# A perceiver layer with 16 experts: the next expert's tokens turned one piece earlier, the last bias added by VectorE, the gate as four column tiles

## The chip, the cores and the metric

The kernel is one program on one core of a Trainium2 chip. The core has five engines with queues of their own: TensorE (PE in the profile; its weight loads are listed as PEld), VectorE (DVE), ScalarE (ACT), GpSimd (POOL) and SyncE (SP), which issues most transfers. An engine works through its queue in order. Results of products land in PSUM, which has eight banks; everything else is in SBUF. The metric is the device time of one execution in microseconds (us); less is better.

## The reference

All values are float32. With `x` of 2 x 512 tokens by 512 and a context of 2 x 8192 by 512, the layer is three residual blocks:

```python
x = x + xattn(layernorm(x), ctx, mask)     # 16 heads over 8192 keys
x = x + window_attn(layernorm(x))          # 16 heads, 7 keys around each token
x = x + ffn(layernorm(x))                  # 16 experts and a shared block
```

The change is in the third. The tokens are flattened to `h`, 1024 x 512. Each of 16 experts picks the 128 tokens that score highest for it:

```python
scores = sigmoid(h @ gate_w.T)                    # 1024 x 16
topk_score, topk_ids = top_k(scores.T, 128)       # for each expert
xin = h[topk_ids]                                 # 16 x 128 x 512
up = einsum('ecd,efd->ecf', xin, up_w) + up_b     # f = 2048
g  = einsum('ecd,efd->ecf', xin, gw) + gb
eo = einsum('ecf,edf->ecd', silu(g) * up, down_w) + down_b
out = zeros.at[topk_ids].add(eo * topk_score)     # a token may be picked by several
shared = (silu(h @ sh_gate_w.T) * (h @ sh_up_w.T)) @ sh_down_w.T
ffn = out + shared
```

## The kernel before, in words

The program is written with tiles and pools. A planner orders the instructions of each engine: it takes them in the order of the source, but one that becomes ready early by its plan may move ahead of earlier source lines. It also puts in all waits. At run time each engine keeps the planned order. So the place of a line in the source is a priority and not a promise.

*Cross attention* (up to line 546) takes most of the span. It is not touched. Its products come in two tile shapes of TensorE that matter below: values `pv` and `av` use 128 rows by 32 columns, four such column tiles beside each other, each writing its own 32 partitions of PSUM; scores `sc` use 32 rows by 128 columns.

*Window attention* (lines 586 to 853) runs over 40 items, batch by head group by block of 103 queries. `beside` (line 776) hangs small work on these items: norms, the transposed `hT` of the tokens, and the preparation of biases. `picks` (784) makes `pick`, 16 blocks of 128 equal columns in which one row is 1 and the others 0. `bias_in` (790) loads `gb` and `up_b` into `rows` and three copies of `down_b` into `raw`; `bias_part` (806) splits `raw` into three bf16 parts, `bias3`, whose sum is the float32 value. So one bf16 product of `pick[:, e, :]` with `bias3` gives 128 equal rows of down's bias for expert e.

*Shared block and gate* (lines 919 to 960). For each batch, eight steps `f` make two products `pf` of 128 x 512 with `hT`, take Silu on ScalarE and multiply into `sT` on VectorE; then four products `pso` over the eight `sT` give the shared output. `gated` (861) runs for both batches after step 5 of batch 0: four products (one per 128 of the model's width) of `gate_sb`, 128 x 16, with 512 tokens, into the first 16 partitions of one bank `pg`, and one Sigmoid into `sc` (16 x 1024). `select` (877) then takes eight of the top 128 scores per call on VectorE, 16 calls hung between the steps; `turned_lists` (890) turns the lists into columns `idx` and `scol`.

*Experts* (lines 962 to 1020). One loop of 65 steps `k`: expert `e`, piece `fq` of four. `expert_in` (962) makes the two products of a piece, `gw` and `up`, each 4 x 4 matmuls of 128 x 128 x 128 into one bank, then four Silus on ScalarE and four joined add-and-multiply on VectorE into `eoT`. `expert_out` (986) of the expert before comes behind piece 0: the bias product (988), 16 matmuls of 512 columns with `down`'s four tiles (994), a multiply by the score column on VectorE (999), and on POOL an indirect transfer that adds the 128 rows to `out` (1000). `gather` (899) fetches the next expert's 128 rows `xin` on POOL in piece 0. `tokens` (908) turns them: `transposed` (95) makes four transposes on TensorE and one copy to `xinT` on ScalarE. Before the change `tokens` stands behind piece 3, so right ahead of the next expert's piece 0, which reads `xinT`.

Weights come through `load_tile` (551) on SyncE's queue: 1 MB each, 12 per expert, into nine buffers in turn (four of `ctx`, five of `w`). A load is issued when the buffer's former tile has been used. `xin`, `xinT`, `eoT`, `sg` and `y` have two buffers each. All results of products take turns in the eight banks of `ps`.

A float32 matmul appears as two records in the trace, a transpose or a bf16 matmul as one.

Of the kernel before, what the change touches and what calls it, by code (L numbers as in the profile page):

```python
# [10 lines left out]
F32 = mybir.dt.float32  # L11
I32 = mybir.dt.int32
U32 = mybir.dt.uint32
BF16 = mybir.dt.bfloat16
AF = mybir.ActivationFunctionType
ALU = mybir.AluOpType
# [3 lines left out]
P = 128  # L20
B, S, D = 2, 512, 512
# [4 lines left out]
DC = D // P  # L26
# [6 lines left out]
E, F, SH, CAP = 16, 2048, 1024, 128  # L33
FQ = F // 512
# [9 lines left out]
def perceiver_kernel(  # L44
# [8 lines left out]
    nc = tc.nc  # L53

    const = ctx.enter_context(tc.tile_pool(name="const", bufs=1))
    ident = const.tile([P, P], F32, name="ident")
# [38 lines left out]
    def transposed(dst, src, ps):  # L95

        tp = ps.tile([P, 4, P], F32, tag="ps", name="tp")
        for c in range(4):
            nc.tensor.transpose(tp[:, c, :], src[:, ts(c, P)], ident)  # L99
        nc.scalar.copy(dst, tp)  # L100
# [17 lines left out]
    with ExitStack() as es:  # L118
        cp = es.enter_context(tc.tile_pool(name="a_const", bufs=1))
        tmp = es.enter_context(tc.tile_pool(name="a_tmp", bufs=2))  # L120
# [8 lines left out]
        ps = first_ps.enter_context(tc.tile_pool(name="a_ps1", bufs=1, space=PSUM))  # L129
# [364 lines left out]
        for slot in range(NS + LAG):  # L494
            if slot == LAG:
                first_ps.close()
                ps = ps_q = es.enter_context(tc.tile_pool(name="a_ps", bufs=8, space=PSUM))
# [53 lines left out]
    def load_tile(src):  # L551
        pool, tag = ((ctxp, "ctx"), (wpool, "w"))[loads[0] % 9 >= 4]
        loads[0] += 1
        t = pool.tile([P, 4, 512], F32, tag=tag, name="wt")
        nc.sync.dma_start(out=t, in_=src)
        return t

    ccp = ctx.enter_context(tc.tile_pool(name="c_const", bufs=1))
    ctmp = ctx.enter_context(tc.tile_pool(name="c_tmp", bufs=2))
    ps = ctx.enter_context(tc.tile_pool(name="c_ps", bufs=8, space=PSUM))  # L560
# [2 lines left out]


    bias_c = ccp.tile([P, 4, P], F32, name="bias_c")


    KB3 = 96
    pick = ccp.tile([KB3, E, P], BF16, name="pick")
    bias3 = ccp.tile([KB3, D], BF16, name="bias3")  # L570
    gate_sb = ccp.tile([P, DC, E], F32, name="gate_sb")
    nc.gpsimd.dma_start(out=gate_sb, in_=gate.rearrange("(c p) e -> p c e", p=P))
    idx = ccp.tile([P, E], U32, name="idx")
    scol = ccp.tile([P, E], F32, name="scol")
# [8 lines left out]
    xnT, aT, hT = {}, {}, {}  # L583


    with ExitStack() as es:
        cp = es.enter_context(tc.tile_pool(name="b_const", bufs=1))
        tmp = es.enter_context(tc.tile_pool(name="b_tmp", bufs=2))
        gp = es.enter_context(tc.tile_pool(name="b_g", bufs=3))
        bp = es.enter_context(tc.tile_pool(name="b_bias", bufs=1))  # L590
# [12 lines left out]
        for h in range(4):  # L603
            r = slice(h * DK, (h + 1) * DK)
# [8 lines left out]
            out=band, in_=band, pattern=[[1, NK]], base=0, channel_multiplier=-1,  # L613
# [3 lines left out]
            out=band, in_=band, pattern=[[-1, NK]], base=W7 - 1, channel_multiplier=1,  # L617
# [3 lines left out]
        def attention_in(n, ln):  # L621
            b, m = divmod(n, NT // B)
            if m == 0:
                xnT[b] = batch_tile("xnT")
            xn = tmp.tile([P, D], F32, tag="row", name="xn")
            normalized(xn, n, *ln)
            transposed(xnT[b][:, :, ts(m, P)], xn, ps)
# [150 lines left out]
        def at(k, f, *args):  # L778
            beside.setdefault(k, []).append(lambda: f(*args))
# [1 line left out]
        def norm(b, key):  # L781
            lns[key] = layernorm_stats(lnp, range(b * (NT // B), (b + 1) * (NT // B)))

        def picks(i):
            r = ds(32 * i, 32)
            nc.vector.tensor_copy(
                pick[r], ident[r, ds(32 * i, E)].unsqueeze(2).to_broadcast([32, E, P])
            )

        def bias_in():  # L790
            rows = bp.tile([P, 4, P], F32, name="rows")
            for i, src in enumerate((gb, up_b)):
                nc.gpsimd.dma_start(
                    out=rows[:, ts(i, 2), :],
                    in_=src.rearrange("e (c p) -> (e c) p", p=P).rearrange("(n r) p -> r n p", r=P),
                )
            raw = bp.tile([KB3, D], F32, name="raw")
            nc.gpsimd.memset(raw, 0.0)
            for i in range(3):
                nc.gpsimd.dma_start(out=raw[ds(32 * i, E), :], in_=down_b)  # L800
            raws.extend((rows, raw))

        def bias_cols():
            transposed(bias_c, raws[0].rearrange("r n p -> r (n p)"), ps)

        def bias_part(i):
            raw = raws[1]
            part = bp.tile([KB3, D], BF16, name="part")
            nc.vector.tensor_copy(part, raw)
            r = ds(32 * i, 32)  # L810
            nc.vector.tensor_copy(bias3[r, :], part[r, :])
            if i < 2:
                nc.vector.tensor_tensor(raw, raw, part, ALU.subtract)

        def forward_in(n, key):

# [8 lines left out]
        lns, raws = {"b0": ln_b0}, []  # L825
        at(2, norm, 1, "b1")
        for i, k in enumerate((4, 6, 8, 10)):
            at(k, lambda n: attention_in(n, lns["b1"]), NT // B + i)
        for i in range(3):
            at(3 + 2 * i, picks, i)  # L830
        at(9, bias_in)
        at(13, bias_cols)
        for i in range(3):
            at(15 + 2 * i, bias_part, i)
        at(29, norm, 0, "f0")
        for i, k in enumerate((31, 33, 35, 37)):
            at(k, forward_in, i, "f0")
# [5 lines left out]
        for k in range(len(items) + 3):  # L843
            i, n = divmod(k, NBQ)
# [14 lines left out]
    sc = sp.tile([E, T], F32, name="sc")  # L859

    def gated(b):
        pg = ps.tile([P, S], F32, tag="ps", name="pg")
        for c in range(DC):
            nc.tensor.matmul(
                pg[0:E, :], lhsT=gate_sb[:, c, :], rhs=hT[b][:, c, :],
                start=(c == 0), stop=(c == DC - 1),
            )
        nc.scalar.activation(sc[:, ts(b, S)], pg[0:E, :], AF.Sigmoid)

# [27 lines left out]
    def gather(e):  # L899

        xin = ep.tile([P, D], F32, name="xin")
        nc.gpsimd.indirect_dma_start(  # L902
            out=xin, out_offset=None, in_=h_dram,
            in_offset=bass.IndirectOffsetOnAxis(ap=idx[:, e : e + 1], axis=0),
        )
        return xin

    def tokens(xin):
        xinT = ep.tile([P, DC, CAP], F32, name="xinT")
        transposed(xinT, xin, ps)  # L910
        return xinT
# [3 lines left out]
    tmp = ctmp  # L915
# [3 lines left out]
    for b in range(B):  # L919
        sT = sTp.tile([P, SH // P, S], F32, tag="sT", name="sT")  # L920
        for f in range(SH // P):
            pair = []
            for wts in (shg, shu):
                pf = ps.tile([P, S], F32, tag="ps", name="pf")
                for c in range(DC):
                    nc.tensor.matmul(  # L926
                        pf, lhsT=wts[f // 4][:, c, ts(f % 4, P)], rhs=hT[b][:, c, :],
                        start=(c == 0), stop=(c == DC - 1),
# [10 lines left out]
            elif b == 1 and f == SH // P - 1:  # L939

                turned_lists()
                xin = gather(0)
# [3 lines left out]
        for j in range(4):  # L946
            po = ps.tile([P, D], F32, tag="ps", name="pso")
            for f in range(SH // P):
                nc.tensor.matmul(  # L949
                    po, lhsT=sT[:, f, ts(j, P)], rhs=shd[f // 4][:, f % 4, :],  # L950
                    start=(f == 0), stop=(f == SH // P - 1),
# [10 lines left out]
    def expert_in(e, fq, xinT, eoT):  # L962

        pair = []
        for src in (gw, up):
            wt = ahead.pop(0) if ahead else load_tile(src[e, fq])
            pf = ps.tile([P, 4, CAP], F32, tag="ps", name="pf")
            for j in range(4):
                for c in range(DC):
                    nc.tensor.matmul(  # L970
                        pf[:, j, :], lhsT=wt[:, c, ts(j, P)], rhs=xinT[:, c, :],
                        start=(c == 0), stop=(c == DC - 1),
                    )
            pair.append(pf)
        sg = tmp.tile([P, 4, CAP], F32, name="sg")
        for j in range(4):
            i, k = divmod(e * (F // P) + fq * 4 + j, P)
            nc.scalar.activation(  # L978
                sg[:, j, :], pair[0][:, j, :], AF.Silu, bias=bias_c[:, i, k : k + 1]
            )  # L980
            nc.vector.scalar_tensor_tensor(  # L981
                eoT[:, fq * 4 + j, :], pair[1][:, j, :], bias_c[:, 2 + i, k : k + 1],
                sg[:, j, :], ALU.add, ALU.mult,
            )

    def expert_out(e, eoT):
        py = ps.tile([P, D], F32, tag="ps", name="py")
        nc.tensor.matmul(
            py, lhsT=pick[:, e, :], rhs=bias3, start=True, stop=False
        )  # L990
        for fq in range(FQ):
            wt = load_tile(down[e, fq])
            for c in range(4):
                nc.tensor.matmul(  # L994
                    py, lhsT=eoT[:, fq * 4 + c, :], rhs=wt[:, c, :],
                    start=False, stop=(fq == FQ - 1 and c == 3),
                )
        y = tmp.tile([P, D], F32, name="y")
        nc.vector.tensor_scalar(y, py, scol[:, e : e + 1], None, ALU.mult)  # L999
        nc.gpsimd.indirect_dma_start(  # L1000
            out=out, out_offset=bass.IndirectOffsetOnAxis(ap=idx[:, e : e + 1], axis=0),
            in_=y, in_offset=None, compute_op=ALU.add,
        )
# [3 lines left out]
    for k in range(E * FQ + 1):  # L1007
        e, fq = divmod(k, FQ)
        if e < E:
            if fq == 0:  # L1010
                eoT[e] = ep.tile([P, F // P, CAP], F32, name="eoT")
                if e > 0:
                    xinT = nxt
                if e + 1 < E:
                    xin = gather(e + 1)
            expert_in(e, fq, xinT, eoT[e])
        if fq == 0 and e > 0:
            expert_out(e - 1, eoT[e - 1])
        if fq == FQ - 1 and e + 1 < E:
            nxt = tokens(xin)  # L1020


# [47 lines left out]
```

## Time and profile before

| what | value |
|---|---|
| median of 3 runs | 3717.26 us (3716.56 to 3718.0) |
| the profiled execution's own time | 3718.25 us |
| its span (first to last instruction) | 3716.5 us |
| TensorE busy | 3669.1 us, 99% |
| VectorE / ScalarE / POOL busy | 2190.0 / 1705.4 / 2083.9 us |
| shared block and gate, on the chain | from about 2831 to 3006 us |
| experts, on the chain | from 3005.77 us to the end |
| weight loads of experts, issue to landing (median) | 5.3 us gw and up, 6.8 us down |
| traffic, expert stretch from 3034 to 3650 | 299 GB/s, transfer engines 87% busy |

The page gives busy times and a chain: the work that ended last, followed backwards to what released each step. A group line has the line of the kernel, engine, operation, result and operands, shape and count; behind the first bar busy time and the mean of one instruction in ns; behind the second the idle time of the engine just before, and what ended it. The chain in order of time has start, duration and what, with the count of instructions. The waits have the waiting line, what it waited for, then total us, times and the longest. Matmuls overlap in the pipeline, so the mean of one matmul is longer than its share of the time; the chain's durations add up.

### The profile page before, as it was taken

The page shows a single profiled execution, that of the slowest core. Times are in us where ns is not written, and L with a number is a line of the kernel's source. Part 1 is how long each engine was busy: PE and PEld are TensorE (multiplying, and loading weights), DVE is VectorE, ACT ScalarE, POOL GpSimd, SP SyncE. Part 2 cuts the span into 40 slices and gives each one's busy share as a digit, 9 for nine tenths or more (in the row PEclk, how much of TensorE's full clock was granted, in tenths as well). Part 3 has the DMA queues.
Part 4 walks back from the last instruction along what each step waited for, and adds up shares of the span by engine and source line. Part 5 has one row for each costly group of instructions (what it writes and reads, how often), then busy time and mean ns, then how long its engine had stood idle before and what let it go on. Part 6 is the DMA issues. An engine that isn't in the chain of part 4 may idle for free.

```text
span 3716.5 us, 108745 instructions
## 1 busy us (share of the span) xinstructions
PE 3669.1 (99%) x47424; PEld 2064.8 (56%) x47424; DVE 2190.0 (59%) x5333; ACT 1705.4 (46%) x3449; POOL 2083.9 (56%) x569
## 2 busy tenths in 40 slices
PE   8999999999999999999999999999999999999998
PEld 4555555555555555555555554444454478888776
DVE  7866667677666766767776676799653711111111
ACT  1145555555555555555555555688463001111110
POOL 0059989998998998999899899700100000000000
PEclk9999999999999999999999999999999999999999
DMA  6322222222224432221222122122201068888885
GB/s 206 104 71 66 73 73 65 66 73 73 65 67 123 124 118 92 73 73 63 69 73 73 61 70 73 61 89 76 76 15 55 34 240 302 299 300 298 300 296 185
DMA packets 145021, 437.88 MB, mean 118 GB/s; under 512 B 9392, under 2 KB 14544, under 8 KB 119200
## 3 DMA queue, kind: packets, MB, share of 16 engines
q1 hardware_dynamic: 139344, 419.20, 34.0%
q0 software_dynamic: 5200, 11.73, 1.2%
q8 instruction: 371, 6.08, 0.7%
q14 instruction: 106, 0.87, 0.1%
HBM read 422.43 MB, written 8.47 MB: 116 GB/s over the span
## 4 chain that ended last, share of the span: by engine, by line
PE 95%; issue 2%; ACT 1%; DMA 1%; POOL 1%; DVE 0%; SPq 0%; POOLq 0%; ACTq 0%
PE av L406 14%; PE sx L318 13%; PE sc L384 12%; PE pk L259 12%; PE pv L277 12%; PE pf L970 12%; PE py L994 6%; PE sc L390 3%; PE pf L926 3%; PE sx L299 2%; PE pqkv L644 2%; PE pso L949 1%; PE po L107 1%; PE pq L185 1%; ACT sb L720 1%
## 5 line engine op out<-in xcount | busy, mean ns | idle before, releaser
L418 POOL TENSOR_TENSOR acc<-acc,pt 128x2048 f32<-128x2048 f32 x437 | 1991.1, 4556 | 168.8 <-ACT pt L397 161.8
L323 DVE CUSTOM_DVE_ANT_0 junk<-sx,mk 128x512 bf16<-128x512 f32 x1776 | 1225.4, 690 | 628.8 <-PE sx L318 432.4
L397 ACT ACTIVATE pt<-sc,mbias 128x512 f32<-128x512 f32 x2016 | 1220.3, 689 | 788.4 <-PE sc L390 788.1
L277 PEld LDWEIGHTS pv<-wv_sb,ctx_t 128*32 128x32 f32 x16384 | 457.6, 110 | 176.5 <-DVE mst L323 103.3
L384 PE MATMUL sc<-qT,kt 32*128 32x512 f32 x4096 | 542.1, 595 | 0.0
L406 PE MATMUL av<-pt,vt 128*32 128x512 f32 x4032 | 539.6, 605 | 0.0
L318 PE MATMUL sx<-kt,qT 32*128 32x512 f32 x3552 | 508.0, 640 | 0.7 <-ACT vt L286 0.7
L277 PE MATMUL pv<-wv_sb,ctx_t 128*32 128x128 f32 x16384 | 500.1, 273 | 2.0 <-DVE avs L414 2.0
L259 PE MATMUL pk<-ctx_t,wk_sb 128*32 128x256 f32 (+1 forms) x9088 | 493.4, 357 | 1.3 <-DMA ctx_t<-in_ctxT 1.3
L970 PE MATMUL pf<-xinT,wt 128*128 128x128 f32 x4096 | 463.9, 275 | 10.1 <-ACT xinT L100 10.1
L970 PEld LDWEIGHTS pf<-xinT,wt 128*128 128x128 f32 x4096 | 461.0, 192 | 21.3 <-ACT xinT L100 13.7
L259 PEld LDWEIGHTS pk<-ctx_t,wk_sb 128*32 128x32 f32 x9088 | 280.6, 110 | 290.1 <-DVE mst L323 100.8
L414 DVE TENSOR_TENSOR avs<-av,avs 128x512 f32<-128x512 f32 x504 | 344.8, 684 | 2.0 <-PE av L406 2.0
L384 PEld LDWEIGHTS sc<-qT,kt 32*128 32x128 f32 x4096 | 234.7, 184 | 188.3 <-issue 111.0
L978 ACT ACTIVATE sg<-pf,bias_c 128x128 f32<-128x128 f32 x256 | 73.0, 368 | 566.3 <-PE pf L970 566.3
L981 DVE SCALAR_TENSOR_TENSOR eoT<-pf,bias_c,sg 128x128 f32<-128x128 f32 x256 | 72.1, 344 | 413.5 <-PE pf L970 413.5
L406 PEld LDWEIGHTS av<-pt,vt 128*32 128x32 f32 x4032 | 80.2, 108 | 323.0 <-DVE mst L323 277.8
L1000 POOL DMA_INDIRECT out_x<-y,idx x16 | 25.2, 1576 | 402.5 <-DVE y L999 402.5
L902 POOL DMA_INDIRECT xin<-h_dram,idx x16 | 15.8, 990 | 411.7 <-PE tp L99 286.6
L263 ACT ACTIVATE kt<-pk,bk_c 128x256 f32<-128x256 f32 (+1 forms) x284 | 128.1, 451 | 209.0 <-PE pk L259 209.0
L994 PE MATMUL py<-wt,eoT 128*128 128x512 f32 x512 | 222.3, 592 | 0.0
L318 PEld LDWEIGHTS sx<-kt,qT 32*128 32x128 f32 x3552 | 139.6, 183 | 135.3 <-issue 70.5
(177 smaller groups left out, 2360.5 us busy)
## 6 DMA issues: line engine op xcount, KB each, us to landing
ctx_t<-in_ctxT SPq DMA_DIRECT2D x159, 1024.0 KB, 6.4
wt<-in_gw SPq DMA_DIRECT2D x64, 1024.0 KB, 5.3
wt<-in_up SPq DMA_DIRECT2D x64, 1024.0 KB, 5.3
wt<-in_down SPq DMA_DIRECT2D x64, 1024.0 KB, 6.8
mk<-mrow SPq DMA_DIRECT2D x111, 256.0 KB, 3.5
ctx<-in_wqkv SPq DMA_DIRECT2D x3, 1024.0 KB, 5.2
mk<-mrow_h SPq DMA_DIRECT2D x16, 128.0 KB, 4.5
wt<-in_sh_d SPq DMA_DIRECT2D x2, 1024.0 KB, 4.8
```

The costliest lines, as they stand in the source:

```text
L259: nc.tensor.matmul(pk[ts(h, DK), :], lhsT=wk_sb[:, c, ds(g * P + h * DK, DK)], rhs=ctx_t[slot, b][:, c, hs], start=(c == 0), stop=(c == DC ...
L263: nc.scalar.activation(k_t[slot][:, hs], pk, AF.Identity, bias=bk_c[:, g : g + 1])
L277: nc.tensor.matmul(pv[ts(k, DK), i, :], lhsT=ctx_t[slot, b][:, c, ds((lo + i) * P + k * DK, DK)], rhs=wv_sb[:, c, ts(g, P)], start=(c == 0 ...
L318: nc.tensor.matmul(sm, lhsT=qT[r, g, ds(b * S + c * P, P)], rhs=k_t[s][r, :], start=True, stop=True)
L323: nc.vector.tensor_tensor_reduce(out=junk, in0=ss[h], in1=mk_t[s], scale=1.0, scalar=-3.0e38, op0=ALU.add, op1=ALU.max, accum_out=mst[u][: ...
L384: nc.tensor.matmul(sc, lhsT=k_t[s][r, ts(ch, P)], rhs=qT[r, g, ts(b, S)], start=True, stop=False)
L397: nc.scalar.activation(pt[:, h, :], ss[h], AF.Exp, bias=mbias[:, b, cc : cc + 1], scale=SCALE)
L406: nc.tensor.matmul(av[ts(h, DK), :], lhsT=v_t[s][:, ch, ts(h, DK)], rhs=pt_t[s, ch][:, h, :], start=True, stop=True,)
L414: nc.vector.tensor_tensor(avs[u], av, avs[u], ALU.add)
L418: eng.tensor_tensor(acc[u], acc[u], pt_t[s, ch], ALU.add)
L970: nc.tensor.matmul(pf[:, j, :], lhsT=wt[:, c, ts(j, P)], rhs=xinT[:, c, :], start=(c == 0), stop=(c == DC - 1),)
L994: nc.tensor.matmul(py, lhsT=eoT[:, fq * 4 + c, :], rhs=wt[:, c, :], start=False, stop=(fq == FQ - 1 and c == 3),)
```

## The change

Three edits go together.

1. `tokens(xin)` for the next expert stands in front of piece 3 instead of behind it.
2. `pick`, `bias3`, their preparation and the bias product go. `expert_out` loads down's bias of its expert as one row repeated to 128 partitions into `y` on SyncE's queue, VectorE multiplies it by the score column, and the last step becomes product times score plus `y`.
3. `gated` computes each batch as four groups of 128 tokens, each in its own 16 of 32 partitions of a 128 x 128 tile, and takes four Sigmoids per batch back into the 16 rows of `sc`.

```diff
-    KB3 = 96
-    pick = ccp.tile([KB3, E, P], BF16, name="pick")
-    bias3 = ccp.tile([KB3, D], BF16, name="bias3")
...
         def bias_in():
...
-            raw = bp.tile([KB3, D], F32, name="raw")
-            nc.gpsimd.memset(raw, 0.0)
-            for i in range(3):
-                nc.gpsimd.dma_start(out=raw[ds(32 * i, E), :], in_=down_b)
-            raws.extend((rows, raw))
+            raws.append(rows)
...
-        for i in range(3):
-            at(3 + 2 * i, picks, i)
         at(9, bias_in)
         at(13, bias_cols)
-        for i in range(3):
-            at(15 + 2 * i, bias_part, i)
...
     def gated(b):
-        pg = ps.tile([P, S], F32, tag="ps", name="pg")
+        pg = ps.tile([P, P], F32, tag="ps", name="pg")
         for c in range(DC):
-            nc.tensor.matmul(
-                pg[0:E, :], lhsT=gate_sb[:, c, :], rhs=hT[b][:, c, :],
-                start=(c == 0), stop=(c == DC - 1),
-            )
-        nc.scalar.activation(sc[:, ts(b, S)], pg[0:E, :], AF.Sigmoid)
+            for m in range(4):
+                nc.tensor.matmul(
+                    pg[ds(32 * m, E), :], lhsT=gate_sb[:, c, :], rhs=hT[b][:, c, ts(m, P)],
+                    start=(c == 0), stop=(c == DC - 1),
+                )
+        for m in range(4):
+            nc.scalar.activation(sc[:, ds(b * S + m * P, P)], pg[ds(32 * m, E), :], AF.Sigmoid)
...
     def expert_out(e, eoT):
         py = ps.tile([P, D], F32, tag="ps", name="py")
-        nc.tensor.matmul(
-            py, lhsT=pick[:, e, :], rhs=bias3, start=True, stop=False
-        )
+        y = tmp.tile([P, D], F32, name="y")
+        nc.sync.dma_start(out=y, in_=down_b[e].partition_broadcast(P))
+        nc.vector.tensor_scalar(y, y, scol[:, e : e + 1], None, ALU.mult)
         for fq in range(FQ):
             wt = load_tile(down[e, fq])
             for c in range(4):
                 nc.tensor.matmul(
                     py, lhsT=eoT[:, fq * 4 + c, :], rhs=wt[:, c, :],
-                    start=False, stop=(fq == FQ - 1 and c == 3),
-                )
-        y = tmp.tile([P, D], F32, name="y")
-        nc.vector.tensor_scalar(y, py, scol[:, e : e + 1], None, ALU.mult)
+                    start=(fq == 0 and c == 0), stop=(fq == FQ - 1 and c == 3),
+                )
+        nc.vector.scalar_tensor_tensor(y, py, scol[:, e : e + 1], y, ALU.mult, ALU.add)
         nc.gpsimd.indirect_dma_start(
...
                 if e + 1 < E:
                     xin = gather(e + 1)
+            if fq == FQ - 1 and e + 1 < E:
+                nxt = tokens(xin)
             expert_in(e, fq, xinT, eoT[e])
         if fq == 0 and e > 0:
             expert_out(e - 1, eoT[e - 1])
-        if fq == FQ - 1 and e + 1 < E:
-            nxt = tokens(xin)
```

More of the change, by code (lines that the diff above doesn't have):

```diff
@@ L782, in norm @@
             lns[key] = layernorm_stats(lnp, range(b * (NT // B), (b + 1) * (NT // B)))
[L784 to L787, printed above, removed]
-            )
         def bias_in():
@@ L796, in bias_in @@
                 )
-            raw = bp.tile([KB3, D], F32, name="raw")
-            nc.gpsimd.memset(raw, 0.0)
-            for i in range(3):
-                nc.gpsimd.dma_start(out=raw[ds(32 * i, E), :], in_=down_b)
-            raws.extend((rows, raw))
+            raws.append(rows)
         def bias_cols():
             transposed(bias_c, raws[0].rearrange("r n p -> r (n p)"), ps)
[L806 to L813, printed above, removed]
         def forward_in(n, key):
```

## The prediction

> **What bounds the kernel now.** I read the page first: busy shares, the slices with the clock, the chain by engine.
>
> ```profile
> PE 3669.1 (99%) x47424; PEld 2064.8 (56%) x47424; DVE 2190.0 (59%) x5333; ACT 1705.4 (46%) x3449; POOL 2083.9 (56%) x569
> PEclk9999999999999999999999999999999999999999
> PE 95%; issue 2%; ACT 1%; DMA 1%; POOL 1%; DVE 0%; SPq 0%; POOLq 0%; ACTq 0%
> ```
>
> TensorE is busy 99% of the span at the full clock and is 95% of the chain that ended last. So a change is worth what it takes from TensorE's own queue. All other engines count only where TensorE waits for them. Second, the chain in order of time over the experts (start, duration, what; each f32 product counts as two records). One period:
>
> ```profile
> 3034.35 0.45 PE tp L99 x4
> 3034.80 0.02 issue
> 3034.82 0.59 ACT xinT L100
> 3035.42 0.04 issue
> 3035.46 7.41 PE pf L970 x64
> 3042.87 0.22 PE py L988
> 3043.09 13.73 PE py L994 x32
> 3056.83 21.44 PE pf L970 x192
> ```
>
> It repeats every 43.92 us (the next turn starts at 3078.26). TensorE stands still once in it: between the four transposes and the next expert's first product, while ScalarE copies xinT. Third, the same view around two products of attention and around the gate:
>
> ```profile
> 2501.49 0.87 PE pv L277 x32
> 2502.36 1.07 PE sc L384 x8
> 2503.65 1.00 PE av L406 x8
> ```
>
> ```profile
> 2874.14 6.97 PE pg L864 x16
> 2881.11 13.93 PE pf L926 x32
> ```
>
> Around the gate TensorE has no gap. Last, the groups of instructions in the expert stretch, SyncE's waits there, its timeline, and TensorE's at the same time:
>
> ```profile
> L970 PE MATMUL pf<-xinT,wt 128*128 128x128 f32 x4094 | 463.7, 275 | 10.1 <-ACT xinT L100 10.1
> L988 PE MATMUL py<-bias,pick 96*128 96x512 bf16 x16 | 6.1, 381 | 0.0
> ```
>
> ```profile
> SPq L555 <- PE pf L970: 395.9, 119, 4.5
> SPq L555 <- PE py L994: 172.5, 56, 3.2
> ```
>
> ```profile
> 3056.86 11.05 SPq L555 DMA_DIRECT2D wt<-in_down  x4
> ```
>
> ```profile
> 3086.84 13.90 PE L994 MATMUL py<-wt,eoT 128*128 128x512 f32 x32
> ```
>
> SyncE waits only for TensorE to free a weight buffer, never TensorE for a transfer. The down tiles issued from 3056.86 are used from 3086.84: 30 us of lead against 6.9 us to land (median of those loads), so 23 us to spare.
>
> **Tokens in front of the last piece.** The step that moves is four transposes on TensorE and one copy on ScalarE; it issues no DMA. On TensorE it passes the 64 records of the last piece; on ScalarE, its four silus; nothing on SP. On POOL the gather two experts on waits for these transposes and starts some 7.1 us earlier. The transposes stay at 0.45 us. What goes is the stall: 0.02 + 0.59 + 0.04 = 0.65 us, and the refill behind it: 64 records took 7.41 us here, but 192 took 21.44, which is 7.15 per 64, so 0.26. Together 0.91 us, 15 times: **-13.7 us**. The copy (0.59) is then covered by the last piece's 7.15 us. Without that cover it costs the same 0.91 again. The gathered rows must be there earlier: those turned at 3078 were gathered at 2999.17, so nothing is late. Low end of the gain: the 10.1 us of idle time alone; high end 13.7, taken because the chain shows the refill in each period.
>
> **Down's bias on VectorE.** Gone are 16 products of 0.22 us on the chain: **-3.5 us** (6.1 by their busy time, but they overlap their neighbours). Added per expert:
> - SyncE issues one more load, one row repeated to 128x512, 256 KB. The nearest row is the mask's rows of the same size, 3.5 us to land. In transfer time: the hardware queue moved 419.20 MB in 34.0% of the span, 3.0 us per MB, so 0.8 us. The engines were busy 0.87 of 43.92 us, 38.2; with this, 39.0 of a new period of 42.78, 0.91. Below one, so nothing; it costs once the load takes over 4.6 us of all engines.
> - VectorE multiplies it by the score: 0.48 us (the 128x512 multiply from SBUF at L429) to 0.75 (L999, from PSUM). VectorE is busy 74 of 616 us there. This waits for the load, and the next piece's products into eoT queue behind it. Those are wanted a piece (7 us) later at the earliest, and two buffers of sg let ScalarE and TensorE run two pieces on, some 14 us. Nothing.
> - The last multiply becomes multiply and add. Only after the final expert is it on the path: 0.75 us at L999, against 0.69 for adding PSUM and SBUF at L111. Between -0.1 and +0.3; I take 0.
>
> Removed earlier: VectorE's picks (three of 1.2 us) and parts (3.5 us in all), POOL's memset and three loads, between 2612 and 2643. VectorE waited 0.48 us for ScalarE right behind the last of them, so they delay no one. TensorE stands still 3.0 us in all between 2632 and 2642, for copies and residuals, so another order of instructions there (the program orders itself by a plan) may be worth -3 to +3 us; I take 0, since no wait names a removed instruction.
>
> **Gate.** 16 records of 512 columns took 6.97 us. Now there are 64 of 128 columns in four column tiles. The nearest row is the value product, 128 rows by 32 columns by 128: 500.1 us for 16384, 30.5 ns each, so 1.95 us. Changing the tile shape has a price: av does the same work as pv but follows another shape, 1.00 against 0.87, and sc 1.07; so 0.13 and 0.20, both once: 0.3. **-4.7 us**. The other end: if the tiles run one after the other, the price is that of pf's 128 columns, 21.44/192 = 0.112 us, 7.1 in all: +0.2.
> Sigmoid becomes eight instructions of 0.285 us (L978: 73.0 us for 256) for two of 0.59. With the table load of 1.28 after the first half, they end near 2878.7 instead of 2881.7. So VectorE's rounds of top 8 start 3.0 us earlier while TensorE is 4.7 ahead. The tightest follower is pso's use of the last sT, written by 2896.63 and needed at 2895.04 + 14/16 x 6.87 = 2901.05: 4.4 us of slack become 2.7. So nothing. The Trainium skill (TensorEngine Tiling, Performance Considerations) says that tiling speeds up TensorE but not the emptying of PSUM, which may then become the bound. That speaks against this edit (second rival).
>
> **Sum.** -13.7 - 3.5 - 4.7 = -21.9 us. The profiled execution took 3718.25 us (span 3716.5), 1.0 above the median of the runs, 3717.26. So 3696.4 in its own time, **3695.4** as a median. 0.2% of it, 7.4 us, is about what a measurement here can tell from no change.
>
> **Rivals.**
> - *The column tiles do not run side by side* (the gate doesn't do what it says). For: 64 weight loads instead of 16, and only 16 of 32 columns used, a shape that this trace lacks. Against: pv and pk keep up 30 and 54 ns with 32 columns. Time: 3695.4 + 4.9 = 3700.3. Chance 0.09.
> - *Emptying the gate's bank becomes the bound*: VectorE starts late, and pso waits for sT. Eight sigmoids at the whole 0.59 us instead of 0.285 would end 2.4 us later, inside the 2.7 us of slack; all 4.7 us are lost only from 7.4 us later: 3700.1. Chance 0.02. By the Trainium skill's rule above this is the likelier course; no row bears it out.
> - *The stall only moves*: the transposes wait in front of the last piece, for a late gather or a bank. For: POOL is in order, and a scatter waiting for y stands between gathers. Against: the gathers were issued 54 us and more before their transposes (2980.53 for 3034.35, the nearest). Time: 3695.4 + 13.7 = 3709.1. Chance 0.05.
> - *SyncE is held by the new load*, which ends slower. There are two y buffers, so y's load must wait until the scatter-add of two experts before has read it. If the plan puts it right behind that scatter, SyncE stands there, and all weight loads behind it, for up to 0.75 (y) + 1.6 (issue) + 5.4 (landing, 10.6 at most) us: 8 to 13. Transfers in flight cover about 5.5 of it. A period is then 39.0 + (hold - 5.5): above 42.78 from a hold of 9.3, and slower than before (14 x 1.56 us lost) from 10.8. At 13: 46.5, 14 x 3.7 = 52 us, 3747. Against: the load stands in the source behind weight loads that are freed some 35 us after that scatter, and the 23 us to spare swallow a hold that is caught up within the period. Chance 0.05. The Trainium skill (DMA: Bandwidth & Descriptors, Anatomy of one DMA) says that any wait on a semaphore is made by the issuing sequencer before dispatch, not by the DMA engines; SyncE's 568 us of waits here agree.
>
> **Chances.** Forecast 0.75, its own range 3691 to 3699: 3.6 up if only the idle 10.1 goes, 4 down for the order around 2640 and the bias products' overlap. With the first two rivals and the +3 us of that order the range is 3690 to 3704, which leaves out the last two rivals and some 0.04 of unnamed ones. Faster by over 0.2% (below 3709.8): 0.91, with the first two rivals and the third, which lies just inside; within 0.2%: 0.04; slower: 0.05.
>
> **What would show it.** Right: no idle time of pf behind ACT xinT; a period of 42.8 us; no product from pick; pg some 2.3 us in the chain, and sc's first reader earlier by 3; SyncE still waiting for TensorE alone. Wrong: TensorE idle behind a wt load, SyncE waiting for the out_x scatter, pf or tp waiting for VectorE, pg near 7 us.

## The result, and the profile after

| | before | after |
|---|---|---|
| median of 4 runs each, side by side | 3717.21 us (3716.56 to 3718.0) | 3694.57 us (3693.85 to 3697.27) |
| the profiled execution's own time | 3718.25 us | 3693.85 us |
| its span | 3716.5 us | 3692.1 us |
| first product of the experts | 3005.77 us | 2999.13 us |
| one expert (period of the chain) | 43.92 us | 42.75 us |

The ratio is 0.9939 with a 95% interval of 0.9924 to 0.9955: faster by 22.6 us, where 21.9 were forecast (3695.4).

The page of the changed kernel, the same three lines as before (busy shares, clock by slice, chain by engine), and one more from the costliest groups over the experts:

```profile
PE 3656.7 (99%) x47456; PEld 2062.0 (56%) x47456; DVE 2189.4 (59%) x5338; ACT 1708.8 (46%) x3455; POOL 2083.0 (56%) x565
PEclk9999999999999999999999999999999999999999
PE 96%; ACT 1%; issue 1%; POOL 1%; DMA 0%; DVE 0%; SPq 0%; POOLq 0%; ACTq 0%
L944 PE MATMUL pf<-xinT,wt 128*128 128x128 f32 x4096 | 462.4, 275 | 0.0
```

TensorE is still the bound, at the full clock. The last line is the one to set against the 10.1 us of idle time that the same products had behind ScalarE's copy: it is 0.0 now.

The chain in order of time over one expert (start, duration, what):

```profile
3020.57 0.44 PE tp L99 x4
3021.01 14.29 PE pf L944 x128
3035.30 13.73 PE py L968 x32
3049.04 14.29 PE pf L944 x128
3063.33 0.44 PE tp L99 x4
3063.76 14.29 PE pf L944 x128
3078.06 13.73 PE py L968 x32
3091.79 14.29 PE pf L944 x128
```

Each `py` now follows `pf` without the product from `pick`, and the transposes stand between two runs of 128 products without a gap on either side. 3091.79 - 3049.04 = 42.75 us. The refill is gone too: 64 records behind the transposes took 7.41 us before, and 128 take 14.29, or 7.15 per 64. The view over a stretch of 640 us (length, busy time and number for PE, PEld, DVE, ACT and POOL, then clock, DMA share, GB/s):

```profile
3000.00:3640.00 640.00, 640.00 (x4420) 529.44 (x4419) 84.62 (x272) 78.58 (x259) 35.06 (x27) 1.00 0.89 312
```

TensorE is busy in all of the 640 us; before it was busy in 630.55 of them.

The chain ahead of the gate (one line) and around it, and ScalarE's and VectorE's timelines behind it (the bracket is the idle time ahead of the instruction and what ended it):

```profile
2829.65 13.73 PE pf L900 x32
2872.61 1.87 PE pg L837 x64
2874.48 13.93 PE pf L900 x32
2888.41 27.47 PE pso L923 x64
```

```profile
2873.70 1.28 ACT L842 ACT_TABLE_LOAD   x1 [3.90 <-PE pg L837]
2875.00 2.25 ACT L842 ACTIVATE sc<-pg 16x128 f32<-16x128 f32 x8
```

```profile
2877.28 1.22 DVE L857 MAX8 top<-sc 16x8 f32<-16x1024 f32 x1 [3.87 <-ACT sc L842]
```

The gate takes 1.87 us instead of 6.97. The 32 `pf` records behind it take 13.93 us, before as after, and 32 such records elsewhere 13.73. The first round of top 8 starts 4.67 us after the gate's start instead of 7.62.

**Where the 24.4 us between the two profiles lie.** The gate starts 1.5 us earlier (2872.61 against 2874.14). It is 5.1 us shorter. From its end to the first product of the experts it is 124.65 us against 124.66, so nothing of that is given back. From the experts' first product to the end of the last `py` it is 683.7 us (2999.13 to 3682.80) against 701.3 (3005.77 to 3707.02): 17.6 less, which is 15 periods of 1.17 us less. What follows the last product takes 9.3 us instead of 9.5. Together 1.5 + 5.1 + 17.6 + 0.2 = 24.4.

**What came otherwise than forecast.** SyncE does wait behind a scatter-add. Its waits in the expert stretch (engine and line, what it waited for: us in all, times, longest):

```profile
SPq L555 <- PE pf L944: 296.7, 102, 3.6
SPq L555 <- PE py L968: 181.6, 60, 3.0
SPq L963 <- DMA out_x<-y,idx: 91.9, 14, 8.1
```

The plan put the load of an expert's `y` almost a period ahead of its place in the source: behind the first of the four `down` loads of the expert before, where it must wait for the scatter-add that frees its buffer. SyncE's timeline shows it:

```profile
3049.07 0.33 SPq L555 DMA_DIRECT2D wt<-in_down  x1
3055.57 0.33 SPq L963 DMA_DIRECT2D y<-in_down_b  x1
3055.99 4.13 SPq L555 DMA_DIRECT2D wt<-in_down  x3
```

So SyncE stands for 6.6 us per expert, 8.1 at most. VectorE's timeline shows the other end of the same hold:

```profile
3049.08 0.75 DVE L972 SCALAR_TENSOR_TENSOR y<-py,scol,y 128x512 f32<-128x512 f32 x1 [12.54 <-PE py L968]
3060.37 0.48 DVE L964 TENSOR_SCALAR y<-y,scol 128x512 f32<-128x512 f32 x1 [10.54 <-DMA y<-in_down_b]
3060.77 1.12 DVE L955 SCALAR_TENSOR_TENSOR eoT<-pf,bias_c,sg 128x128 f32<-128x128 f32 x4
```

VectorE waits 10.54 us for `y`, and four multiplies into `eoT` come in one go behind it. TensorE does not feel either. The Trainium skill (DMA: Bandwidth & Descriptors, Anatomy of one DMA) says that a wait on a semaphore is made on the issuing sequencer, ahead of dispatch; the 91.9 us of SyncE's line L963 agree. Whether such a wait costs anything is what the experiments ask.

### The profile page after: what moved, and what is told of

The parts are those of the page before. It is cut to its first block, busy times and chain, and to the rows that moved or that the text cites. A ratio compares the mean times of both kernels' runs of the same rounds, so it can differ in the third digit from the quotient of the medians.

```text
span 3692.1 us, 108872 instructions
## 1 busy us (share of the span) xinstructions
PE 3656.7 (99%) x47456; PEld 2062.0 (56%) x47456; DVE 2189.4 (59%) x5338; ACT 1708.8 (46%) x3455; POOL 2083.0 (56%) x565
## 4 chain that ended last, share of the span: by engine, by line
PE 96%; ACT 1%; issue 1%; POOL 1%; DMA 0%; DVE 0%; SPq 0%; POOLq 0%; ACTq 0%
PE av L406 14%; PE sx L318 13%; PE sc L384 12%; PE pk L259 12%; PE pv L277 12%; PE pf L944 12%; PE py L968 6%; PE pf L900 3%; PE sc L390 3%; PE sx L299 2%; PE pqkv L639 2%; PE po L107 2%; PE pso L923 1%; PE pq L185 1%; ACT sb L715 1%
## 5 line engine op out<-in xcount | busy, mean ns | idle before, releaser
L390 PE MATMUL sc<-mT,neg 32*128 32x512 bf16 x2048 | 204.3, 374 | 0.0
```

The lines of the kernel that those rows point to most:

```text
L390: nc.tensor.matmul(ss[h], lhsT=neg[r, :], rhs=m_t[u][r, :], start=False, stop=True)
```

## The experiments

Each ran beside the kernel before on its chip: 3716.41 us for the first four, 3717.33 for the next four, 3717.12 for the last three. Ratios are to that, with 95% intervals.

### One edit at a time

The three edits were each made alone on the kernel before.

**Tokens only**

```diff
+            if fq == FQ - 1 and e + 1 < E:
+                nxt = tokens(xin)
             expert_in(e, fq, xinT, eoT[e])
         if fq == 0 and e > 0:
             expert_out(e - 1, eoT[e - 1])
-        if fq == FQ - 1 and e + 1 < E:
-            nxt = tokens(xin)
```

> The kernel before with only the tokens turned in front of piece 3; bias product and gate as before. My theory: the stall of 0.65 us and the refill of 0.26 us go from 15 of the periods, nothing else changes: 13.7 us less than before (ratio 0.9963), a period of 43.0 us (43.92 - 0.91), no idle time of pf behind ACT xinT. Rival, the refill was no cost of the stall: 10.1 us less, a period of 43.25. Rival, the edit needs the others (the bias product between the pieces sets the pace): little or nothing.

Measured: 3703.09 us, ratio 0.9962 (0.9948 to 0.9975), so 13.3 us less. Its chain, one period:

```profile
3171.08 0.22 PE py L988
3171.30 13.74 PE py L994 x32
3185.03 14.29 PE pf L970 x128
3199.32 0.44 PE tp L99 x4
3199.76 14.29 PE pf L970 x128
3214.05 0.22 PE py L988
```

The period is 42.97 us, 0.95 below that of before, with the bias product (0.22) still in it. Fifteen times 0.95 is 14.3. The stall of 0.65 and the refill of 0.26 are both gone and nothing has come in their place.

**Bias only** (the preparation of `pick` and `bias3` goes too)

```diff
...
-        nc.tensor.matmul(
-            py, lhsT=pick[:, e, :], rhs=bias3, start=True, stop=False
-        )
+        y = tmp.tile([P, D], F32, name="y")
+        nc.sync.dma_start(out=y, in_=down_b[e].partition_broadcast(P))
+        nc.vector.tensor_scalar(y, y, scol[:, e : e + 1], None, ALU.mult)
...
-        nc.vector.tensor_scalar(y, py, scol[:, e : e + 1], None, ALU.mult)
+        nc.vector.scalar_tensor_tensor(y, py, scol[:, e : e + 1], y, ALU.mult, ALU.add)
...
```

> The kernel before with only down's bias as a repeated row; tokens and gate as before. My theory: 16 products of 0.22 us go and the load, its wait on SyncE and VectorE's multiply cost nothing: 3.5 us less than before (ratio 0.9991), a period of 43.70 us. Rival, the products cost their full busy time of 0.38: 6.1 us less. Rival, SyncE's waiting for the scatter-add costs something: less than 3.5 us gained, or a loss, and TensorE idle behind wt loads.

Measured: 3714.24 us, ratio 0.9992 (0.9983 to 1.0001), so 2.2 us less. Its period is 43.69 us (3166.34 to 3210.03): 0.23 less than before, the whole of the removed product. The time alone does not settle whether 3.5 us arrive, as the interval is 6.7 us wide; the last set of runs comes back to it.

**Gate only**

```diff
-            nc.tensor.matmul(
-                pg[0:E, :], lhsT=gate_sb[:, c, :], rhs=hT[b][:, c, :],
...
+            for m in range(4):
+                nc.tensor.matmul(
+                    pg[ds(32 * m, E), :], lhsT=gate_sb[:, c, :], rhs=hT[b][:, c, ts(m, P)],
...
```

> The kernel before with only the gate as four column tiles. My theory: pg takes 1.9 us in the chain as in the changed kernel, instead of 6.97, and no one gives it back: 5.1 us less than before (ratio 0.9986); VectorE's first top 8 starts 3 us earlier. Rival, TensorE gets ahead of VectorE and waits at pso for sT: less than 5.1, up to nothing, with idle time of pso behind DVE.

Measured: 3711.89 us, ratio 0.9989 (0.998 to 0.9998), so 4.5 us less. The chain has the same line as the changed kernel:

```profile
2872.96 1.87 PE pg L865 x64
```

The three alone give 13.3 + 2.2 + 4.5 = 20.0 us, against 22.6 together. The spread of each is some 1 to 3 us, so the difference shows no interaction. The periods and the gate's line need none.

### Is it the tiles side by side?

The changed kernel with the gate's 64 records kept, but all groups in the same 16 partitions, at four places of a bank. The two loops change places as well, so that one group is finished before the next:

```diff
-        pg = ps.tile([P, P], F32, tag="ps", name="pg")
-        for c in range(DC):
-            for m in range(4):
+        pg = ps.tile([P, 4, P], F32, tag="ps", name="pg")
+        for m in range(4):
+            for c in range(DC):
                 nc.tensor.matmul(
-                    pg[ds(32 * m, E), :], lhsT=gate_sb[:, c, :], rhs=hT[b][:, c, ts(m, P)],
+                    pg[0:E, m, :], lhsT=gate_sb[:, c, :], rhs=hT[b][:, c, ts(m, P)],
...
```

> The changed kernel, but the gate's four groups of 128 tokens are written to the same 16 partitions, at four places of the bank, so that no column tiles lie beside each other; the number and size of the products and of the sigmoids stay. My theory: the gain of the gate is the tiles running side by side, so 64 records take 0.112 us each, 7.1 us, 5.3 us more than the changed kernel: 22.7 - 5.3 = 17.4 us less than before (ratio 0.9953). Rival, the gain is from smaller products or from 16 columns of weights: as fast as the changed kernel, ratio 0.9939.

Measured: 3701.3 us, ratio 0.9956 (0.9942 to 0.997), so 15.1 us less than before, not 22.6. On the chain:

```profile
2875.53 7.09 PE pg L837 x64
```

The same 64 records take 7.09 us when they share their columns and 1.87 in four column tiles: 111 ns each against 29. By itself this leaves open whether the order of the loops has a part in it. TensorE's timelines of the first moments settle that. First the changed kernel from 2872.5 to 2872.65, then this one from 2875.4 to 2875.65:

```profile
2872.54 0.30 PE L837 MATMUL pg<-hT,gate_sb 128*16 128x128 f32 x4
```

```profile
2875.46 0.39 PE L837 MATMUL pg<-hT,gate_sb 128*16 128x128 f32 x2
```

In four column tiles four records start within 0.02 us, and a new set of four follows every 0.11 us; in the same partitions a single record starts every 0.11 us. So the gain of the gate comes from the tiles working side by side, and smaller products or 16 columns of weights alone give nothing: 7.09 us is no less than the 6.97 of before.

The medians differ by 6.7 us and the two profiled spans by 8.2. Of the 8.2, 5.2 are the gate and 2.9 the later start of the gate in this execution.

### Does the held SyncE cost anything?

**The load of y on POOL's queue**

```diff
-        nc.sync.dma_start(out=y, in_=down_b[e].partition_broadcast(P))
+        nc.gpsimd.dma_start(out=y, in_=down_b[e].partition_broadcast(P))
```

> The changed kernel, but the repeated row is loaded from POOL's queue instead of SyncE's, so that no weight load stands behind the wait for the scatter-add. In the changed kernel SyncE is held 92 us in all by it (14 times, 6.6 us each). My theory: the lead of the weight loads swallows this hold, so the time is that of the changed kernel, ratio 0.9939 to the kernel before, within 0.0005; SyncE waits for TensorE alone. Rival, the hold costs TensorE something that the chain does not name: some us faster, up to 14 x 1 us.

Measured: 3693.93 us (3693.06 to 3695.15), ratio 0.9936 (0.9923 to 0.995). SyncE now waits for TensorE alone, and the wait stands in POOL's queue:

```profile
SPq L555 <- PE pf L944: 395.1, 123, 3.6
SPq L555 <- PE py L968: 181.6, 60, 3.0
```

```profile
POOL y L963 <- DMA out_x<-y,idx: 60.7, 14, 5.0
```

With the hold taken from SyncE the time is the same within the spread, and so is the period (42.76 us). SyncE's waits for `pf` are 395.1 us here and 296.7 with the hold. So the hold only took the place of waiting for TensorE that SyncE does anyway, and the 91.9 us cost nothing that these runs can tell.

**The hold made longer.** Behind each scatter-add, two narrow indirect writes that also read `y`, four in a second kernel; the buffer is free only when these have landed:

```diff
+        for _ in range(2):
+            nc.gpsimd.indirect_dma_start(
+                out=scratch, out_offset=bass.IndirectOffsetOnAxis(ap=idx[:, e : e + 1], axis=0),
+                in_=y[:, 0:16], in_offset=None,
+            )
```

> The changed kernel with two more indirect writes of 16 columns of y to a scratch table behind each scatter-add, so that y's buffer comes free later and SyncE is held longer; the output is not touched by them. By my price a period is 39.0 us of transfers plus the hold less 5.5 us, if that is more than 42.75. Two writes should lengthen the hold from 6.6 to some 13 us, less what the planner moves the load back for: a period of at most 46.5, up to 14 x 3.7 = 52 us slower than the changed kernel; no change if the hold stays under 9.3 us. Rival, the nine buffers' lead of 23 us is what counts and not the transfer rate: no change.

> As the kernel with two more writes, but four. The hold should grow to some 20 to 25 us. By my price (39.0 + hold - 5.5 per period) a period of 54 to 58 us, 150 to 215 us slower than the changed kernel. VectorE's multiply is held by the same load, and the two pieces of cover (14 us) behind it are then used up as well, so TensorE would wait for weights or for VectorE. Rival, the lead swallows it: no change, or a few us.

Measured: 3700.75 us with two, ratio 0.9957 (0.9942 to 0.9972), and 3700.14 with four, ratio 0.9954 (0.9939 to 0.997): 6 us above the changed kernel in both. But the six are not in the experts. The chain of the kernel with four over one of them:

```profile
3078.25 13.73 PE py L969 x32
3091.99 14.29 PE pf L945 x128
3106.28 0.44 PE tp L99 x4
3106.72 14.29 PE pf L945 x128
3121.01 4.29 PE py L969 x10
```

The period is 42.76 us. The last `py` ends at 3682.27 us with two and 3683.01 with four, against 3682.80 without them. What follows takes 16.0 and 15.2 us instead of 9.3: the extra writes behind the very last scatter-add.

The hold did not grow as much as the writes were meant to make it. SyncE's and VectorE's waits with four:

```profile
SPq L964 <- DMA scratch<-y,idx: 103.8, 14, 11.9
```

```profile
DVE y L965 <- DMA y<-in_down_b: 161.5, 14, 12.8
```

That is 7.4 us each (7.7 with two, 115.5 us in 15 waits), because the plan moved the load of `y` further back: behind one `down` load in the changed kernel, two with two writes, four with four. So the forecasts of a period of 46.5 and of 54 to 58 us were not put to the test. Single holds of up to 11.9 us occurred, beyond the 9.3 from which the prediction's formula would have a loss if every period had one. SyncE catches up by issuing the loads that have come free meanwhile one after another:

```profile
3113.94 0.33 SPq L964 DMA_DIRECT2D y<-in_down_b  x1
3114.40 0.34 SPq L555 DMA_DIRECT2D wt<-in_gw  x1
3114.84 0.38 SPq L555 DMA_DIRECT2D wt<-in_up  x1
3115.31 0.38 SPq L555 DMA_DIRECT2D wt<-in_gw  x1
3117.47 0.33 SPq L555 DMA_DIRECT2D wt<-in_up  x1
```

The transfers follow in bursts. The rate of the DMA engines over the expert stretch, in 40 slices, first the changed kernel, then the one with four writes:

```profile
GB/s 287 308 305 275 349 298 318 327 270 354 296 328 317 269 358 295 341 307 277 348 294 330 321 278 345 290 311 336 235 395 291 330 321 272 343 286 326 309 194 1
```

```profile
GB/s 286 310 301 302 239 374 205 383 365 185 421 231 397 344 195 415 218 393 346 197 417 200 362 398 221 397 193 376 397 197 409 213 399 351 210 382 191 376 269 2
```

A slice at 200 GB/s is followed by one at 400, and both kernels move the same 197.93 MB by the hardware queue there, with TensorE never idle. The records of the loads and of the products show what paid for the hold. From the issue of a weight load to the first product that reads its tile pass at least 28.0 us in the kernel before, 23.4 in the changed kernel and 18.9 with four writes. In the repeat of the changed kernel at the end of this section, no tile lands less than 15.9 us before it is read. So a hold is paid from the lead of the buffers, which is back at some 28 us before the next one. Where a steady hold begins to cost was not reached.

### Can the order in the window stage give more?

The norm and the transposes for the shared block moved five items earlier:

```diff
-        at(29, norm, 0, "f0")
-        for i, k in enumerate((31, 33, 35, 37)):
+        at(24, norm, 0, "f0")
+        for i, k in enumerate((25, 27, 29, 31)):
```

> The changed kernel with the second block's norm and the transposed tokens of batch 0 hung five items earlier (24 to 31 instead of 29 to 37), so that the shared block's first products are ready while TensorE waits at the end of window attention, 2801 to 2815. My theory: TensorE's waits there (some 5 us in the changed kernel's trace) are filled by these products if the planner moves them up: 3 to 5 us faster than the changed kernel, ratio 0.993. Rival, the planner leaves them behind the window's last products, in the source's order: no change.

Measured: 3694.01 us (3693.35 to 3696.36), ratio 0.9938 (0.9924 to 0.9951): no change. The shared products still follow the window's last ones:

```profile
2813.44 15.77 PE po L107 x32
2829.20 13.73 PE pf L900 x32
```

### What the bias edit is worth inside the whole, and what its added work costs

Three kernels beside each other: the kernel before with the tokens' step and the gate's tiles but the old bias (both diffs above); the changed kernel with no bias at all; the changed kernel once more. The second:

```diff
-        nc.sync.dma_start(out=y, in_=down_b[e].partition_broadcast(P))
-        nc.vector.tensor_scalar(y, y, scol[:, e : e + 1], None, ALU.mult)
...
-        nc.vector.scalar_tensor_tensor(y, py, scol[:, e : e + 1], y, ALU.mult, ALU.add)
+        nc.vector.tensor_scalar(y, py, scol[:, e : e + 1], None, ALU.mult)
```

> The kernel before with the tokens' step and the gate's four column tiles, and the bias still added by TensorE's product. It measures what the bias edit is worth inside the whole change, since alone it gave 2.2 us, with an interval about as wide as that. Theory (sixteen products of 0.22 us are what goes): 3.5 us slower than the changed kernel, so 3698.1, and a period of 42.97 us against 42.75. Rival (the edit alone showed its whole worth; part of the 3.5 is given back somewhere): some 2 us slower, 3696.6, with the same difference of the periods. Rival (the edit's removal of the rows and picks earlier brings a time of its own): more than 5 us slower, with TensorE's products before the gate starting some 2 us later than in the changed kernel.

> The changed kernel without down's bias: y's load and its multiply are left out, and the last step is a multiply alone, so the bias is missing from the output. It measures what the added load, the hold of SyncE and VectorE's multiply cost together. Theory (all of it is hidden): the same as the changed kernel, 3693.9, within its spread of 1.5 us, with a period of 42.75 us, SyncE waiting for TensorE alone and a DMA share near 0.87. Rival (the repeated row costs transfer time that TensorE feels, 0.1 to 0.2 us per expert): 2 to 3 us faster, 3691 to 3692, with a shorter period.

> The changed kernel once more, beside the two others on the same chip. All theories: 3694 us, between 3692.5 and 3697.5. It gives the other two a neighbour, and one more profile in which the start of the gate can be set against the run before: if its earlier start (2872.61 against 2874.14 us) is a part of the change, it shows again within 0.3 us; if it is a difference from execution to execution, it lies anywhere between 2872 and 2876.

| | median | ratio | span of the profile | gate's start | period |
|---|---|---|---|---|---|
| without the bias edit | 3698.71 us (3697.66 to 3701.23) | 0.9951 (0.9937 to 0.9964) | 3697.0 | 2873.87 | 42.97 |
| no bias at all | 3695.32 us (3693.9 to 3698.83) | 0.9943 (0.993 to 0.9957) | 3692.7 | 2873.29 | 42.76 |
| the changed kernel again | 3694.01 us (3693.23 to 3698.37) | 0.9941 (0.9928 to 0.9955) | 3691.6 | 2872.10 | 42.75 |

Without the edit the time is 4.7 us above the changed kernel. The periods differ by 0.22, the forecast's price, which makes 3.5; the two spans differ by 5.4, and of the 1.9 beyond 3.5 the gate's later start is 1.8. So the theory's 3.5 is right within the experts, and the rest belongs to the stretch ahead of the gate. The medians alone would not tell 3.5 from 2 or 5, as the runs of each kernel spread over 3.6 and 5.1 us.

Leaving the bias out altogether gains nothing more. The period is the same, so the load, SyncE's hold, VectorE's wait and its multiply together cost nothing within the experts. The windowed view of the kernel without bias:

```profile
3000.00:3640.00 640.00, 640.00 (x4425) 529.75 (x4424) 79.76 (x259) 78.35 (x259) 35.03 (x27) 1.00 0.89 306
```

The DMA share is 0.89 with the repeated row and 0.89 without. The expectation of 0.87 here was wrong: the rise from 0.87 comes from the shorter period alone (0.87 x 43.92 / 42.76 = 0.894).

The gate's start did not come back within 0.3 us in the changed kernel's second profile: 2872.10 against 2872.61, and its `po` ahead of the gate took 15.27 us against 16.50. Over all thirteen profiles of this study the gate starts between 2872.06 and 2875.53 us. The nine with the bias edit span that whole range, the four without it 2872.96 to 2874.36. So the 1.5 us of the first comparison can't be given to the change. Whether a part of it (under 1 us by the means, 2873.2 and 2873.8) belongs to the removed preparation stays open.

## Why the prediction was right, point by point

- **TensorE's queue is the bound, so a change is worth what it takes from there.** Right. Of the 24.4 us between the profiles, 22.7 are shown on TensorE's chain at the two places that the forecast named, the experts and the gate. That the medians came within 0.7 us of the forecast is partly luck, as the interval of the ratio is 11.5 us wide; the period and the gate's line are the better test, and by them no term is more than 0.6 us off.
- **Tokens, -13.7.** Right. 13.3 alone by the clock; 0.95 per period against the forecast's 0.91. The cover held: the copy to `xinT` is under the last piece's products, and no product waits for it.
- **Bias, -3.5.** Right in size: 0.22 per period in both directions (added alone, taken from the whole). The time with it alone, 2.2, could not show it. The terms set at nothing were nothing, as the kernel without bias shows. But two of their reasons were off. The 0.8 us of transfer time for the repeated row was too high: the DMA share did not rise at all beyond the shorter period's effect (0.89, not 0.91; two decimals leave room for 0.4 us). And the load did not stand behind the weight loads that precede it in the source. L429, which the prediction calls a multiply, is an addition; the multiply itself (L964) took the same 0.48 us.
- **Gate, -4.7.** Right, and the price was better than forecast: 1.87 us where 1.95 + 0.3 had been worked out. The 0.3 for changes of the tile shape, taken from `av` and `sc`, is the mis-sized term. There is such a price, but the kernel before pays it already: its 16 gate records and the 32 `pf` records behind them take 6.97 + 13.93 us, and as many `pf` records elsewhere 6.87 + 13.73, so 0.3 less. The 0.2 behind the gate is there in both kernels and so is no cost of the change. The Trainium skill (TensorEngine Tiling, Tiling Modes, Key Properties) says that a change of tiling mode drains TensorE. Whether the 0.2 us are such a drain is not shown: they are the same with 512 columns, with four column tiles and with all groups in the same partitions. The start of the top 8 moved by 2.95 us (forecast 3.0).
- **Emptying the bank as the bound.** Did not happen. The last `sT` is written at 2890.94 and needed at 2888.41 + 14/16 x 6.87 = 2894.42, so 3.5 us of slack are left (forecast 2.7). The prediction called this the likelier course by the Trainium skill (TensorEngine Tiling, Performance Considerations); the Trainium skill says there only that emptying PSUM may become the bound. Here the eight Sigmoids took 2.25 us and no product waited for one.
- **Window stage, 0 within -3 to +3.** Not contradicted, and more can't be said: what differs there from profile to profile of one kernel is of the size of the term.
- **Tiles not side by side.** False; shown by the kernel with groups in the same partitions, 5.2 us longer on the chain (forecast of that rival 4.9).
- **SyncE is held by y's load.** Its first half came true and its second did not. The sign "SyncE still waiting for TensorE alone" failed, and "SyncE waiting for the out_x scatter", listed as a sign of being wrong, came true: the plan put the load where it waits for the scatter-add. The hold was 6.6 us and not 8 to 13, and the lead of nine weight buffers swallowed it, which the prediction's own sentence on the 23 us to spare had said. The rival's point of decision, a hold of 9.3 us in every period, stays untested: the mean reached 7.7 us, and single holds of 11.9 us cost nothing.

## What to carry to other kernels

When one engine is busy for 99% of the span, sum what leaves its own chain, stall and refill, and check the other engines only for a wait that reaches it; here that gave 21.9 us forecast for 22.6 measured. A long wait in another engine's queue is not a cost by itself: compare it with the lead of the buffers behind it, and see whether the queue issues its backlog at once afterwards. For a product with few output columns, try the groups in column tiles that run beside each other, here 3.8 times as fast; to see that it is the tiles, run the same number of records in one.

## What the runs showed that had not been expected

- Sixteen-column weights with 128 moving columns in four column tiles run at 29 ns per record, 3.8 times the rate of the same records in one place (111 ns). The products of 128 columns behind them take 0.2 us more than elsewhere, and just as much behind the gate of before.
- A row repeated to 128 partitions, 256 KB, once per 42.75 us, raised the rate from 306 to 312 GB/s and the DMA share not at all.
- The same instructions ahead of the gate (`po`, 32 records) took between 15.17 and 16.66 us from profile to profile; why was not found out.
